# Softmax groups computed from PSUM with row sums on ScalarE, in a cross-attention kernel with a hand-written order

## The chip, the cores and the metric

The kernel runs on one core of a Trainium2 chip. The metric is device time in microseconds (us), the median over several executions. A core has five engines with a queue each: TensorE (PE in the profile; its weight loads are PEld), VectorE (DVE), ScalarE (ACT), GpSimd (POOL) and SyncE (SP), which here issues nearly all DMAs. Each queue runs in order; between engines semaphores wait for data and for buffers to come free. PE writes its results to PSUM, which has 8 banks of 128 x 512 floats; everything else lives in SBUF.

## The reference

Cross-attention with two key sets (77 text keys and 77 image keys, each with a softmax of its own), 20 heads of 32, for 2 x 2048 tokens of width 640, all in fp32:

```python
q = _split_heads(hidden_states @ Wq.T, H)
k = _split_heads(text @ Wk.T, H);     v = _split_heads(text @ Wv.T, H)
k_ip = _split_heads(ip @ Wk_ip.T, H); v_ip = _split_heads(ip @ Wv_ip.T, H)
out = _merge_heads(_attend(q, k, v, sm_scale)) + _merge_heads(_attend(q, k_ip, v_ip, sm_scale))
out = out @ Wo.T + bo
return out + residual
```

`_attend` is softmax(q k^T * sm_scale) v.

## The kernel before

The work is cut into 20 units u: 2 batches x 5 chunks of 128 channels (4 heads) x 2 halves of 1024 tokens. Two units with the same batch and chunk make a pair, numbered 0 to 9. A unit's 8 token tiles fall into three softmax groups s: groups 0 and 1 of three tiles (3 tiles x 4 heads x 2 key sets = 24 softmax rows of 77 for each token), group 2 of two tiles (16 rows). The text writes (u, s) for a group.

For each unit and 512 tokens PE projects the queries (`queries`, L197, into one bank) and ACT takes them out (L207). For each group PE computes the scores (`scores`, L229) into one half of PSUM: four banks, one for each head. Then follow, word for word of the order below:

- K: ACT copies the four banks to `pb` in SBUF (`take`, L241), after which the half is free.
- M: DVE takes the row maxima (`maxima`, L268 from SBUF, L271 from PSUM).
- S: POOL subtracts them from the rows (`subtract`, L282); E: ACT takes the exponential of the whole group in one instruction (`exponential`, L288).
- Groups in `BIASED` leave S out: the maxima are negated, and ACT takes each row by itself with its maximum as the bias (`exponential_of`, L257), 24 or 16 instructions. Groups in `DIRECT` (one before) leave K out too: maxima and exponentials read PSUM.
- D: DVE sums the rows (L295) and takes reciprocals (L297); N: POOL multiplies (`normalise`, L302); T: DVE transposes in blocks of 32 (L309).

Then PE attends for the pair (A, `attend`, L318, into one half), and ACT takes the result to `aT` (L341, L345). Keys and values of each chunk are projected (k and v, `project_kv`, L138), the values transposed by DVE (SQ, L148) and spread over `v4` by 2 x 8 small DMAs (VS, L154). The output projection of batch 0 runs under the attention of batch 1: seven block products for each 512 tokens (m1 to m7, `product`, L476 and L486, added by DVE into `acc`, L501 and L507, words cm) and a last chunk of 128 channels (o, L457, added into `res`, L467). `acc` and `res` are loaded with the residual (SF), filled and stored (SS), once for each 512 tokens. Batch 1 has a scheme of 33 products at the very end (F, L830), with weights and token sums made by DVE and POOL (V and X, L810 and L816) and results added by DVE (Y, L774 and L776).

Nothing schedules this at build time. `SCHEDULE` is one long string of words; `emit` issues each word's instructions in turn, so the words of one engine stand in its queue in that order. In `R1.13@0` the part before the dot is the word and group, then comes the unit, then the PSUM half; for q, k, v, o, p, m and F the number after @ is a bank. LX loads a block of x (1,280 KB) into one of three buffers and waits for the queries that read it, LQ and LK load weights, LO the output weights `wo_ct`. All of these are in SP's queue. The DMAs use eight semaphores in turn, so a DMA can also wait for the one issued eight before it.

Of the kernel before, what the change touches and what calls it, by code (L numbers as in the profile page):

```python
# [9 lines left out]
F32 = mybir.dt.float32  # L10
# [10 lines left out]
def kernel(  # L21
# [43 lines left out]
        (1, 2),  # L65
    }
    BIASED = {
        (1, 0), (2, 2), (3, 2), (5, 2), (6, 2), (8, 2), (9, 2), (10, 2), (11, 2), (12, 0), (12, 2), (13, 2),
        (14, 2), (15, 1), (15, 2), (16, 2), (17, 2), (18, 2), (19, 2),
# [149 lines left out]
    def rows_of(u, s):  # L219
        return keys_of(u, s).rearrange("p n g (t l) -> p (n g) t l", l=L)  # L220
# [29 lines left out]
    def exponential_of(u, s, ps=None):  # L250

        n = GROUPS[s][1]
        for g in range(G):
            for t in range(n):
                for x in range(2):
                    row = rows_of(u, s)[:, t * G + g, x]
                    nc.scalar.activation(  # L257
                        row,
                        row if ps is None else rows_in(ps[g], n)[:, t, x],
                        AF.Exp,  # L260
                        bias=maxs[(u, s)][:, t * G + g, x : x + 1],
                    )
# [29 lines left out]
    def sums(u, s):  # L292
        n = GROUPS[s][1] * G
        den = small.tile([P, n, 2], F32, tag=f"den{n}", name=f"den_{u}_{s}")
        nc.vector.tensor_reduce(den, rows_of(u, s), AX.X, ALU.add)  # L295
        rden = small.tile([P, n, 2], F32, tag=f"rden{n}", name=f"rden_{u}_{s}")
        nc.vector.reciprocal(rden, den)  # L297
        rdens[(u, s)] = rden
# [241 lines left out]
    for t in range(2):  # L540
# [75 lines left out]
    def emit(word):  # L616
# [24 lines left out]
        elif k == "SF":  # L641
            fetch(x, PARTS[y])
        elif k == "SS":
            store(x, PARTS[y])
        elif k[0] in "KMSEDNT":
            ps = at[f"R{i}.{x}"]
            if k[0] == "K":
                take(x, i, ps)
# [224 lines left out]
```

## Time and profile before

| what | us |
|---|---|
| median of 3 runs | 503.95 (503.49 to 506.41) |
| the profiled execution | 506.55 |
| its span, first to last instruction | 504.8 |

The profile is that of one execution. Each engine's busy time is given with its share of the span; a group of instructions is named by its line in the kernel, with the tile written and the tile read, the number of instructions, their busy time together, the mean time of one, and the idle time before them with what ended it. On PE an fp32 matmul shows as two instructions. The mean time of one instruction is from its start to its end; where neighbours overlap, busy time divided by the count is less, and that is what a queue of them takes. The chain of waits goes back from the last instruction to whatever released each step.

DVE's other large items, beside those that the prediction quotes, are the transposes (115.7 us in all), POOL's the normalisation (176.1) and the subtraction (128.3).

### The profile page before, as it was taken

The page shows a single profiled execution, that of the slowest core. Times are in us where ns is not written, and L with a number is a line of the kernel's source. Part 1 is how long each engine was busy: PE and PEld are TensorE (multiplying, and loading weights), DVE is VectorE, ACT ScalarE, POOL GpSimd, SP SyncE. Part 2 cuts the span into 40 slices and gives each one's busy share as a digit, 9 for nine tenths or more (in the row PEclk, how much of TensorE's full clock was granted, in tenths as well). Part 3 has the DMA queues.
Part 4 walks back from the last instruction along what each step waited for, and adds up shares of the span by engine and source line. Part 5 has one row for each costly group of instructions (what it writes and reads, how often), then busy time and mean ns, then how long its engine had stood idle before and what let it go on. Part 6 is the DMA issues. An engine that isn't in the chain of part 4 may idle for free.

```text
span 504.8 us, 10180 instructions
## 1 busy us (share of the span) xinstructions
PE 494.1 (98%) x4114; PEld 290.5 (58%) x4114; DVE 431.5 (85%) x397; ACT 299.0 (59%) x743; POOL 379.8 (75%) x163
## 2 busy tenths in 40 slices
PE   8999999999999999999999999999999999999996
PEld 4657567648557556456566556555665675443442
DVE  0069999989998999869999899788899989898985
ACT  1169788768787589658786947586786354100000
POOL 0069588998898887789886888459789979797530
PEclk9999999999999999999999999999999999999999
DMA  8981351230491471885423773454545104310125
GB/s 268 354 223 43 93 138 39 70 84 12 133 259 38 126 254 31 283 297 187 133 62 93 228 255 99 149 178 147 181 133 174 43 2 147 126 62 22 42 93 199
DMA packets 67471, 69.37 MB, mean 137 GB/s; under 512 B 5472, under 2 KB 47200, under 8 KB 67424
## 3 DMA queue, kind: packets, MB, share of 16 engines
q1 hardware_dynamic: 66704, 68.00, 43.2%
q8 instruction: 32, 0.52, 0.4%
q10 hardware_dynamic: 720, 0.72, 0.4%
q14 instruction: 15, 0.12, 0.1%
HBM read 54.94 MB, written 10.49 MB: 130 GB/s over the span
## 4 chain that ended last, share of the span: by engine, by line
PE 82%; DMA 10%; DVE 3%; SPq 3%; issue 1%; ACT 1%; DVEq 0%
PE bank L197 29%; PE bank L318 10%; PE bank L476 9%; PE bank L830 9%; PE bank L229 9%; PE bank L138 8%; PE bank L457 6%; DMA wo_ct<-in_L_xattn_Wo_dram 3%; PE bank L486 3%; DMA out_dram<-res 2%; DMA aT<-in_L_xattn_Wk_ip_dram 2%; DMA wq<-in_L_xattn_Wq_dram 1%; DMA x<-in_x_dram 1%; DVE x L776 1%; SPq L154 1%
## 5 line engine op out<-in xcount | busy, mean ns | idle before, releaser
L302 POOL TENSOR_TENSOR pb<-pb,rden 128x1848 f32<-128x1848 f32 (+1 forms) x60 | 176.1, 2942 | 36.8 <-DVE rden L297 34.9
L197 PE MATMUL bank<-x,wq 128*128 128x512 f32 x400 | 180.8, 601 | 1.3 <-DMA x<-in_x_dram 1.1
L282 POOL TENSOR_TENSOR pb<-pb,mx 128x1848 f32<-128x1848 f32 (+1 forms) x40 | 128.3, 3210 | 52.0 <-DVE mx L268 51.8
L268 DVE TENSOR_REDUCE mx<-pb 128x24 f32<-128x1848 f32 (+1 forms) x59 | 108.2, 1845 | 33.3 <-ACT pb L241 33.1
L197 PEld LDWEIGHTS bank<-x,wq 128*128 128x128 f32 x400 | 74.0, 191 | 88.0 <-issue 81.4
L295 DVE TENSOR_REDUCE den<-pb 128x24 f32<-128x1848 f32 (+1 forms) x60 | 110.4, 1840 | 14.9 <-ACT pb L288 13.8
L309 DVE STREAM_TRANSPOSE pb<-pb 128x1920 f32<-128x1920 f32 (+1 forms) x60 | 115.7, 1931 | 5.2 <-POOL pb L302 4.7
L241 ACT COPY pb<-bank 128x462 f32<-128x462 f32 (+1 forms) x236 | 100.2, 533 | 32.9 <-PE bank L229 32.3
L288 ACT ACTIVATE pb<-pb 128x1848 f32<-128x1848 f32 (+1 forms) x40 | 68.4, 1714 | 34.0 <-POOL pb L282 33.8
L257 ACT ACTIVATE pb<-pb,mx 128x77 f32<-128x77 f32 x328 | 84.0, 356 | 6.8 <-DVE mx L268 6.7
L229 PEld LDWEIGHTS bank<-kT,qT 32*128 32x128 f32 x1280 | 46.2, 184 | 24.9 <-issue 16.0
L229 PE MATMUL bank<-kT,qT 32*128 32x154 f32 x1280 | 57.6, 306 | 0.5 <-ACT kT L545 0.3
L318 PE MATMUL bank<-pb,v 32*32 32x512 f32 x1600 | 56.7, 597 | 0.9 <-issue 0.7
L138 PEld LDWEIGHTS bank<-wo_ct,aT 128*128 128x128 f32 x320 | 43.4, 188 | 5.5 <-issue 4.6
L138 PE MATMUL bank<-wo_ct,aT 128*128 128x154 f32 x320 | 45.9, 296 | 0.1
L318 PEld LDWEIGHTS bank<-pb,v 32*32 32x32 f32 x1600 | 31.5, 103 | 22.4 <-issue 10.3
L207 ACT ACTIVATE qT<-bank 128x512 f32<-128x512 f32 x40 | 23.7, 600 | 32.9 <-PE bank L197 32.9
L457 PE MATMUL bank<-aT,wo_ct 128*128 128x512 f32 x80 | 36.4, 597 | 0.1
L476 PE MATMUL bank<-aT,wo_ct 128*128 128x256 f32 x128 | 32.6, 387 | 1.2 <-DVE acc L507 1.2
L476 PEld LDWEIGHTS bank<-aT,wo_ct 128*128 128x128 f32 x128 | 23.5, 190 | 10.3 <-issue 5.0
L776 DVE TENSOR_TENSOR x<-x,bank 128x512 f32<-128x512 f32 x36 | 23.7, 681 | 4.9 <-PE bank L830 4.5
L457 PEld LDWEIGHTS bank<-aT,wo_ct 128*128 128x128 f32 x80 | 14.9, 190 | 17.0 <-issue 16.5
(74 smaller groups left out, 370.3 us busy)
## 6 DMA issues: line engine op xcount, KB each, us to landing
x<-in_x_dram SPq DMA_DIRECT2D x20, 1280.0 KB, 7.7
out_dram<-acc SPq DMA_DIRECT2D x20, 256.0 KB, 2.8
x<-in_x_dram SPq DMA_DIRECT2D x18, 256.0 KB, 5.9
acc<-in_x_dram SPq DMA_DIRECT2D x16, 256.0 KB, 3.8
out_dram<-x SPq DMA_DIRECT2D x15, 256.0 KB, 2.1
v<-vS SPq DMA_DIRECT2D x160, 20.0 KB, 2.4
wq<-in_L_xattn_Wq_dram SPq DMA_DIRECT2D x9, 320.0 KB, 6.8
aT<-in_L_xattn_Wk_dram SPq DMA_DIRECT2D x5, 512.0 KB, 5.4
```

The source lines that it names most:

```text
L138: nc.tensor.matmul(keys_in(out), loaded[n][:, k, :], cT[:, k, :, t, :], start=(k == 0), stop=(k == NCC - 1))
L197: nc.tensor.matmul(pq, wqs[q % 3][:, k, :], xs[place_of(u, h)][:, k, :], start=(k == 0), stop=(k == NC - 1),)
L229: nc.tensor.matmul(ps[g][:, ts(t, 2 * L)], qTs[(u, h)][g * D : (g + 1) * D, ts(st, P)], kT[g * D : (g + 1) * D, c, b].rearrange("p t l -> ...
L241: nc.scalar.copy(keys_of(u, s)[:, :, g], ps[g][:, : n * 2 * L].rearrange("p (n l) -> p n l", n=n))
L257: nc.scalar.activation(row, row if ps is None else rows_in(ps[g], n)[:, t, x], AF.Exp, bias=maxs[(u, s)][:, t * G + g, x : x + 1],)
L268: nc.vector.tensor_reduce(mx, rows_of(u, s), AX.X, ALU.max, negate=negate)
L282: nc.gpsimd.tensor_tensor(rows_of(u, s), rows_of(u, s), maxs[(u, s)].unsqueeze(3).to_broadcast([P, n, 2, L]), ALU.subtract)
L295: nc.vector.tensor_reduce(den, rows_of(u, s), AX.X, ALU.add)
L302: nc.gpsimd.tensor_tensor(rows_of(u, s), rows_of(u, s), rdens[(u, s)].unsqueeze(3).to_broadcast([P, n, 2, L]), ALU.mult)
L309: nc.vector.transpose(p, p)
L318: nc.tensor.matmul(pa[r][g * D : (g + 1) * D, :], v4s[q % 2][rows, g, k, :], zones[rows, :, g, k, :], start=(k == 0), stop=(k == NK - 1),)
L476: nc.tensor.matmul(part, w_of[m][:, kp, op], t_of(m, b, i)[:, kp], start=(op == kp == 0 and m in (1, 2, 5)), stop=(op == 1 and kp == 1 and ...
```

## The change

`DIRECT` grows from one group to ten, all in units 11 to 18; `BIASED` shrinks from 19 groups to 11; and a new set, `SUMMED`, names 11 of these 21 groups whose row sums come out of the exponentials themselves: each L267 instruction gets `accum_out`, which writes the sum of its 77 results. These groups have no D. The reciprocal becomes a word of its own, I (`invert`), for all 60 groups. Line numbers shift by 2 to 16.

```diff
     DIRECT = {
-        (1, 2),
+        (11, 0), (12, 0), (13, 0), (13, 2), (14, 0), (14, 2), (15, 1), (15, 2), (16, 2), (18, 1),
     }
     BIASED = {
-        (1, 0), (2, 2), (3, 2), (5, 2), (6, 2), (8, 2), (9, 2), (10, 2), (11, 2), (12, 0), (12, 2), (13, 2),
-        (14, 2), (15, 1), (15, 2), (16, 2), (17, 2), (18, 2), (19, 2),
+        (3, 2), (4, 0), (5, 2), (6, 2), (8, 2), (9, 2), (10, 2), (11, 2), (12, 2), (18, 2), (19, 2),
+    }
+    SUMMED = {
+        (10, 2), (12, 0), (12, 2), (13, 0), (13, 2), (14, 0), (15, 1), (16, 2), (18, 1), (18, 2), (19, 2),
     }
...
-    def exponential_of(u, s, ps=None):
+    def exponential_of(u, s, ps=None, den=None):
...
                     nc.scalar.activation(
                         row,
                         row if ps is None else rows_in(ps[g], n)[:, t, x],
                         AF.Exp,
-                        bias=maxs[(u, s)][:, t * G + g, x : x + 1],
+                        bias=maxs[(u, s)][:, *one],
+                        accum_out=None if den is None else den[:, *one],
                     )
...
     def sums(u, s):
+        nc.vector.tensor_reduce(den_of(u, s), rows_of(u, s), AX.X, ALU.add)
+
+    def invert(u, s):
         n = GROUPS[s][1] * G
-        den = small.tile([P, n, 2], F32, tag=f"den{n}", name=f"den_{u}_{s}")
-        nc.vector.tensor_reduce(den, rows_of(u, s), AX.X, ALU.add)
         rden = small.tile([P, n, 2], F32, tag=f"rden{n}", name=f"rden_{u}_{s}")
-        nc.vector.reciprocal(rden, den)
+        nc.vector.reciprocal(rden, dens[(u, s)])
...
     SCHEDULE = (
-        "R0.0@1 K0.0 M0.0 LK.4 LK.5 S0.0 R1.0@0 K1.0 M1.0 S1.0 R2.0@1 K2.0 M2.0 S2.0 q.1.1@1 q.1.0@6 v.0.1@0 E0.0 "
...
+        "R0.0@1 R1.0@0 K0.0 q.1.0@4 K1.0 M0.0 M1.0 S0.0 R2.0@0 v.0.0@7 K2.0 cq.1.0 S1.0 M2.0 E0.0 v.0.1@3 LK.6 "
...
     ).split()
```

All of `SCHEDULE` is new. PE's words are the same 231 in both, in another order and partly in other banks; so are the loads and stores, and the words V and X of the last stage are partly moved between DVE and POOL. The three places at which the prediction needs the new order are shown there: PE at the start, SP around A.4 (`VS.4.1 VS.5.1 LO` now follow `LX.12.0 LX.12.1`; before, the order was `LX.12.0 LO VS.4.0 LX.12.1`), and ACT around the group (13, 0).

Between the scores of a direct group and the next use of the banks that they fill, PE's words are now:

```text
R0.11@1  m2.0 o.0                      R1.11@1
R0.12@0  q.13.1 m6.0 q.14.0            A.5@0
R0.13@0  m7.0 q.14.1 m4.0              R1.13@0
R2.13@1  o.1                           m1.1@5 (one bank)
R2.14@0  q.16.0                        R1.14@0
R0.14@0  q.15.1 q.15.0                 A.6@0
R2.15@0  m6.1 q.16.1                   R1.15@0
R1.15@0  m7.1 q.17.0 m4.1 m2.2 R1.16   R0.16@0
R2.16@0  m1.2 q.18.0                   A.7@0
R1.18@0  o.3 q.19.1 m4.2               A.8@0
```

More of the change, by code (lines that the diff above doesn't have):

```diff
@@ L248, in rows_in, with den_of @@
         return ps[:, : n * 2 * L].rearrange("p (n t l) -> p n t l", n=n, t=2)
-    def exponential_of(u, s, ps=None):
+    dens = {}
+    def den_of(u, s):
+        n = GROUPS[s][1] * G
+        dens[(u, s)] = small.tile([P, n, 2], F32, tag=f"den{n}", name=f"den_{u}_{s}")
+        return dens[(u, s)]
+    def exponential_of(u, s, ps=None, den=None):
         n = GROUPS[s][1]
@@ L256, in exponential_of @@
                     row = rows_of(u, s)[:, t * G + g, x]
+                    one = t * G + g, slice(x, x + 1)
                     nc.scalar.activation(
@@ L644, in emit @@
             store(x, PARTS[y])
-        elif k[0] in "KMSEDNT":
+        elif k[0] in "KMSEDINT":
             ps = at[f"R{i}.{x}"]
@@ L653, in emit @@
                 elif direct or biased:
-                    exponential_of(x, i, ps if direct else None)
+                    exponential_of(
+                        x, i, ps if direct else None, den_of(x, i) if (x, i) in SUMMED else None
+                    )
                 else:
@@ L657, in emit @@
             else:
-                dict(S=subtract, D=sums, N=normalise, T=transpose)[k[0]](x, i)
+                dict(S=subtract, D=sums, I=invert, N=normalise, T=transpose)[k[0]](x, i)
         elif k == "q":
```

122 rows, old and new, of the table SCHEDULE are left out of this document.

## The prediction

> **What bounds the kernel now.** I read the page first, for the engines' shares; then the chain of waits, for the price of each kind of work on TensorE; then the waits of PE, and the timeline where they fall.
>
> ```profile
> PE 494.1 (98%) x4114; PEld 290.5 (58%) x4114; DVE 431.5 (85%) x397; ACT 299.0 (59%) x743; POOL 379.8 (75%) x163
> x<-in_x_dram SPq DMA_DIRECT2D x20, 1280.0 KB, 7.7
> ```
>
> PE is busy nearly throughout, so the end moves only by the PE work or by the gaps in it. The chain of waits (start, length, what) prices the work:
>
> ```profile
> 25.59 2.77 ACT pb L241 x6
> 28.40 8.85 PE bank L197 x20
> ...
> 43.65 4.29 PE bank L197 x10
> 47.94 2.11 PE bank L138 x16
> 50.05 0.74 PE bank L229 x16
> 50.78 4.49 PE bank L197 x10
> ...
> 63.39 1.00 PE bank L229 x24
> ...
> 70.98 5.45 PE bank L318 x154
> ...
> 190.29 2.63 DMA v<-vS
> ...
> 201.62 13.02 DMA wo_ct<-in_L_xattn_Wo_dram
> ...
> 214.66 0.51 SPq L154
> ...
> 215.26 6.36 DMA x<-in_x_dram
> ...
> 232.64 0.43 PE bank L486 x2
> 233.07 0.86 PE bank L476 x4
> ...
> 310.88 8.10 DMA out_dram<-res
> 319.04 3.01 DMA res<-in_x_dram
> 322.15 0.75 DVE res L467
> ...
> 414.84 3.43 PE bank L457 x8
> ...
> 446.26 14.61 PE bank L830 x34
> ...
> 500.82 0.69 DVE x L776
> ```
>
> One query projection (q) costs 4.29, one key or value projection 2.11, a group's scores (R) 1.00 or 0.74, an attend (A) 5.45, an output chunk 4.29 (ten instructions like a q) or 3.43, L476, L486 and L830 0.215, 0.215 and 0.43 an instruction. A full-array piece straight behind scores or an attend takes 0.2 more (4.49 against 4.29). From the first scores on the schedule holds 37 q (158.7), 18 projections (38.0), 60 R (54.8), 10 A (54.5), 4 o and 4 p (30.9), 4 z (3.4), 288 instructions of L476 and L486 (61.9) and 132 of L830 (56.8): 459, and 50 changes from scores or attend to full array, 10: 469. Before and after hold the same pieces and, counted in their PE order, the same 50 changes. The timeline has the first scores at 24.5, the chain the last addition at 500.8: 476.3, so 7.4 us are gaps. PE's waits (total, times, longest), and then the timeline (start, length, what, the wait before it), say where:
>
> ```profile
> PE bank L476 <- DVE acc L507: 1.2, 1, 1.2
> PE bank L830 <- DVE pb L810: 1.2, 1, 1.2
> ...
> PE bank L318 <- issue: 0.7, 1, 0.7
> ...
> PE bank L830 <- DVE x L776: 0.3, 1, 0.3
> ```
>
> ```profile
> 24.48 3.81 PE L229 MATMUL bank<-kT,qT 32*128 32x154 f32 x64 [0.31 <-ACT kT L545]
> ...
> 182.89 5.50 PE L318 MATMUL bank<-pb,v 32*32 32x512 f32 x159
> ...
> 209.24 4.56 PE L197 MATMUL bank<-x,wq 128*128 128x512 f32 x10
> 213.73 1.07 PE L229 MATMUL bank<-kT,qT 32*128 32x154 f32 x24
> 214.95 6.40 PE L318 MATMUL bank<-pb,v 32*32 32x512 f32 x160 [0.15 <-DMA v<-vS]
> 221.76 4.53 PE L197 MATMUL bank<-x,wq 128*128 128x512 f32 x10 [0.42 <-DMA x<-in_x_dram]
> ```
>
> The first three score groups take 3.9 (24.48 to 28.40) for 2.74 of work: 1.15 of gap, in which the chain runs through ACT's copies (25.59). A.4 loses 0.15 and 0.9 (6.40 against 5.50), the q behind it 0.42; a product waits 1.2 at 323; the last stage 1.5. That names 6.1 of the 7.4.
>
> **The change part by part.** On PE at the start, of before, from the middle of the third score group (banks 71 to 74):
>
> ```order
> L229 MATMUL bank_71<-kT,qT_1_153 128x154
> L229 MATMUL bank_72<-kT,qT_1_153 128x154
> L229 MATMUL bank_73<-kT,qT_1_153 128x154
> L229 MATMUL bank_74<-kT,qT_1_153 128x154
> L197 MATMUL bank_68<-x_85,wq_75 128x512 x5
> L197 MATMUL bank_73<-x_84,wq_75 128x512 x5
> L138 MATMUL bank_67<-wo_ct,aT 128x154 x8
> ```
>
> And of after, from the last score of the second group (bank 70):
>
> ```order
> L231 MATMUL bank_70<-kT,qT_1_153 128x154
> L199 MATMUL bank_71<-x_84,wq_75 128x512 x5
> L231 MATMUL bank_67<-kT,qT_1_153 128x154
> L231 MATMUL bank_68<-kT,qT_1_153 128x154
> L231 MATMUL bank_69<-kT,qT_1_153 128x154
> ```
>
> A q now stands ahead of the third group: 4.29 us against the 4 copies that must empty its banks. The q itself needs one copied bank, 0.5 us after the first group, while the second group's 1.0 runs. So -1.15.
>
> On SyncE around A.4 (x_83 and x_84 are blocks for the q behind it, v the values for A.4, wo_ct the output weights), of before:
>
> ```order
> L445 DMA res<-in_x_dram 128x512
> L182 DMA x_83<-in_x_dram 128x5x512
> L160 DMA wo_ct<-in_L_xattn_Wo_dram 128x5x640
> L154 DMA v_0_80<-vS_0_93 32x160 x8
> L182 DMA x_84<-in_x_dram 128x5x512
> L182 DMA x_82<-in_x_dram 128x5x512
> ```
>
> and of after:
>
> ```order
> L190 DMA wq_75<-in_L_xattn_Wq_dram 128x5x128
> L184 DMA x_83<-in_x_dram 128x5x512
> L184 DMA x_84<-in_x_dram 128x5x512
> L156 DMA v_0_80<-vS_0_93 32x160 x8
> L156 DMA v_1_81<-vS_95 32x160 x8
> L162 DMA wo_ct<-in_L_xattn_Wo_dram 128x5x640
> ```
>
> In before the last copy of v issues at 214.66, when wo_ct has landed, and x_84 behind it at 215.26; that is the gap of 1.47. Both now stand ahead of wo_ct. The price: x_84 issues once q.11.0, which reads its buffer, ends, 11.7 us of PE work before A.4 (two q 8.58, scores 2.74, changes 0.4). If the last v copy again waits for the big load ahead of it, it goes out at 7.7 (the page's landing time), takes 0.5 to issue and 2.6 to land: 0.9 to spare. wo_ct issues behind 8 more copies of 0.6, 13 us after q.11.0, and is first read 22.9 after it. Its 1.6 MB took 13.0 with 1.3 MB of x just ahead of it, so about 7 alone: 2 to 3 to spare. So -1.5; if the cover is gone, the same 1.5 comes back here.
>
> The product's wait at 323 hangs on res (stored, 8.10, then reloaded, 3.01) behind x blocks. SyncE now stores and reloads it further ahead of its use, so -1.2. The last stage keeps its 1.5: same products, other sequence, no better reason.
>
> The groups need their prices per engine (busy, mean):
>
> ```profile
> L257 ACT ACTIVATE pb<-pb,mx 128x77 f32<-128x77 f32 x328 | 84.0, 356 | 6.8 <-DVE mx L268 6.7
> L257 ACT ACTIVATE pb<-bank,mx 128x77 f32<-128x77 f32 x16 | 3.6, 382 | 0.0
> L271 DVE TENSOR_REDUCE mx<-bank 128x4 f32<-128x308 f32 x4 | 1.6, 455 | 0.0
> L295 DVE TENSOR_REDUCE den<-pb 128x24 f32<-128x1848 f32 x40 | 82.2, 2056 | 11.3 <-ACT pb L288 11.3
> L295 DVE TENSOR_REDUCE den<-pb 128x16 f32<-128x1232 f32 x20 | 28.2, 1409 | 3.6 <-ACT pb L288 2.6 <-ACT pb L257 1.0
> ```
>
> ACT around (13, 0) in before: qT is a query tile, L241 the copies that empty banks, L288 the exponential of a group at once:
>
> ```order
> L207 ACTIVATE qT_1_2437<-bank_72 128x512
> L241 COPY pb<-bank_67 128x3x154
> L241 COPY pb<-bank_68 128x3x154
> L241 COPY pb<-bank_69 128x3x154
> L241 COPY pb<-bank_70 128x3x154
> L241 COPY pb<-bank_71 128x2x154
> L241 COPY pb<-bank_72 128x2x154
> L241 COPY pb<-bank_73 128x2x154
> L241 COPY pb<-bank_74 128x2x154
> L288 ACTIVATE pb<-pb 128x12x154
> ```
>
> and in after:
>
> ```order
> L267 ACTIVATE pb,den_0_2401<-bank_67,mx_0_2396 128x77 x6
> L267 ACTIVATE pb,den_0_2401<-bank_68,mx_0_2396 128x77 x6
> L267 ACTIVATE pb,den_0_2401<-bank_69,mx_0_2396 128x77 x6
> L267 ACTIVATE pb,den_0_2401<-bank_70,mx_0_2396 128x77 x6
> L209 ACTIVATE qT_1_2455<-bank_73 128x512
> L209 ACTIVATE qT_0_2462<-bank_74 128x512
> ```
>
> The group's copies are gone; its banks stay full until the maxima (DVE) and 24 exponentials are through. Maxima from PSUM: 4 x 0.4 for 16 rows, times 2056/1409 (the same reduction's two sizes) for 24: 1.6 and 2.3. A row from PSUM 3.6/16 = 0.225, from SBUF 84.0/328 = 0.256. With 0.2 for two hand-overs a direct group holds its half 5.4 (16) or 7.9 us (24), plus its rows times **a**, the unknown price of a row sum. PE's cover until the half is needed (0.25 more until its last bank): (11,0) m2.0, o.0 7.3; (12,0) 10.8; (13,0) 9.0; (14,2) one q 4.7; (14,0) two q 9.0; (15,2) 6.5; (16,2) 6.5; (18,1) 11.6; (15,1) 12.6. For (13,2) the product behind o.1 needs its second bank alone, and that fits. Without a, (11,0) overruns by 0.6 and (14,2) by 0.7: +1.3.
>
> For a the trace of before shows nothing. From 0 (the sum rides along) to 0.256 (a second instruction like the row); below 0 is excluded, the same row runs. A row takes 356 ns by itself and 256 in the run, so losing the overlap costs 0.10. I take half of that, 0.05: (13,0) and (14,0) then overrun by 0.1 each, +0.2. At 0.10 it is +3.1, at 0.256 +21.
>
> The Trainium skill, ScalarE: Activation LUTs, section Rules for kernel authors, budgets about 0.3 us for an ACTIVATE with a pointer bias plus 0.83 ns an element, which speaks against row by row. By it, an estimate, a row would be 0.36, the overruns would sum to 14 and the kernel would take about 514. The trace disagrees (0.256 and 0.225 in the run), since neighbours overlap, so this gets no chance of its own.
>
> Off the path: DVE loses 11 sums (5 x 2.06 + 6 x 1.41 = 18.7) and gains 2.4 for maxima from PSUM; ACT loses the copies of ten groups. Neither is what PE waits for, so they count nothing. The reciprocals stay 60; one of a summed group now waits for ACT's last row, and behind that of (13, 0), for one, stand a product's addition, a transpose and the maxima of (13, 2) in DVE's queue, for which ACT's next rows and PE's q.16.0 wait. A late row passes its delay to them (rival 2).
>
> Sum on the profiled execution's 506.55 (span 504.8): -1.15 - 1.5 - 1.2 + 1.3 + 0.2 = 504.2. The median of the runs (503.95) lies 2.6 under that execution: 501.6.
>
> **The rivals.** 1. *Row sums are dear* (slower): the read-out is an instruction of its own on ACT, PSUM halves stay full, PE waits at (13,0), (14,0), (16,2), (12,0), (18,1). At a = 0.256: 501.4 + 21 = 522; slower by 1% from a = 0.16 on. For: five covers are within 1 to 4 us of the hold. Against: only five places. The Trainium skill, VectorE: DVE Perf Modes, section Two Vector instructions with no wait between them, says that an op that writes its accumulator is two instructions, of VectorE; no run here shows it yet.
>
> 2. *DVE comes late.* Until A.4 no sum leaves DVE, which is as full as before:
>
> ```profile
> 40.00:60.00 20.00, 20.00 (x163) 13.76 (x156) 19.47 (x21) 18.65 (x62) 13.70 (x5) 1.00 0.25 69
> ```
>
> With 0.5 of 20 free, one transpose or maximum in the wrong place delays an attend or a copy-out; about 1 us at five attends: 506.5, slower than 509 only at 1.5 each. For: every queue is reordered. Against: the same load ran with gaps of 0.7 before.
>
> 3. *Nearly all gaps close* (faster): 506.55 - 7.4 - 2.6 = 496.5 at best, 498.5 with 2 us of gaps left. For: the named gaps are order, not work. Against: the last stage's waits have the same cause as before.
>
> **How the numbers follow.** Forecast 0.42 (own range 499 to 504), rival 1 0.18, rival 2 0.17, rival 3 0.23. About 1% is what a measurement of this kernel tells from no change: 498.9 and 509. Faster: rival 3 and the forecast's edge, 0.25. Slower: most of rival 1, a fourth of rival 2, 0.19. The rest 0.56. The range 496.5 to 510 holds rival 3 and the forecast; it leaves out rival 1 beyond a = 0.17 and the worst of rival 2, 0.16 together.
>
> **What would show it.** Right: PE's first three score groups end without a wait on L241; A.4 takes 5.5; L267 rows with sums run at 0.28 to 0.30; waits of PE's scores on L267 sum to 1 to 2. Wrong: rows with sums at 0.4 or more (rival 1), attends waiting for L309's transposes (rival 2), a v copy or wo_ct landing late at A.4 or m2.0.

## The result, and the profile after

The changed kernel takes 500.36 us (median of 15 runs, 498.81 to 503.98), the kernel before on the same chip 504.54 (15 runs, 503.44 to 506.48): 0.9917 of it, 95% interval 0.9897 to 0.9937. The profiled execution took 503.08 with a span of 501.3. The page's busy times, of the changed kernel:

```profile
PE 492.2 (98%) x4114; PEld 290.7 (58%) x4114; DVE 410.7 (82%) x409; ACT 306.8 (61%) x970; POOL 376.5 (75%) x166
```

VectorE has 21 us less to do than before, ScalarE 8 more. The timeline of PE (start, length, what, and in brackets the wait before it), at the places of which the prediction spoke:

```profile
23.55 1.96 PE L231 MATMUL bank<-kT,qT 32*128 32x154 f32 x48 [0.31 <-ACT kT L557]
25.43 4.56 PE L199 MATMUL bank<-x,wq 128*128 128x512 f32 x10
29.92 0.81 PE L231 MATMUL bank<-kT,qT 32*128 32x154 f32 x16
...
187.03 0.58 PE L231 MATMUL bank<-kT,qT 32*128 32x154 f32 x7 [2.38 <-issue]
187.54 6.06 PE L140 MATMUL bank<-wo_ct,aT 128*128 128x154 f32 x32
...
215.30 5.52 PE L330 MATMUL bank<-pb,v 32*32 32x512 f32 x160
220.75 4.56 PE L199 MATMUL bank<-x,wq 128*128 128x512 f32 x10
...
226.95 1.13 PE L488 MATMUL bank<-aT,wo_ct 128*128 128x256 f32 x4 [0.65 <-DMA wo_ct<-in_L_xattn_Wo_dram]
...
327.97 1.99 PE L488 MATMUL bank<-aT,wo_ct 128*128 128x256 f32 x8
```

The third score group at the start goes straight through behind a q. The attend A.4 (215.30) takes 5.52 and the q behind it has no wait. The product that waited 1.2 for `acc` has none (327.97). What is left is a stop of 2.38 in the middle of a score group, for which the records name no cause, slow projections behind it (6.06 for 32 instructions, 4.48 in an undisturbed execution, below), 0.65 for `wo_ct`, and, not shown here, 0.38 for kT at 57. The view of PE's waits has none for a row of a direct group (L267). The chain of waits, of the changed kernel, ends so:

```profile
203.94 9.47 DMA x<-in_x_dram
...
219.77 7.14 DMA wo_ct<-in_L_xattn_Wo_dram
...
448.55 48.99 PE bank L846 x114
497.56 0.69 DVE acc L792
```

In the last 49 us the chain is PE's own work. From the first scores to the last addition there are 497.56 - 23.55 = 474.0 us, 5.0 over the 469 of work by the prediction's count (7.4 before); 2.38 + 1.58 + 0.65 + 0.38 are those 5.0. The stop is no fixed part of the kernel: two more executions with a profile (below) had 1.00 and 0.63 there, and the projections at full speed.

### The profile page after: what moved, and what is told of

Same layout as the page of the kernel before. It is cut to its first block, busy times and chain, and to the rows that moved or that the text cites. A ratio compares the mean times of both kernels' runs of the same rounds, so it can differ in the third digit from the quotient of the medians.

```text
span 501.3 us, 10439 instructions
## 1 busy us (share of the span) xinstructions
PE 492.2 (98%) x4114; PEld 290.7 (58%) x4114; DVE 410.7 (82%) x409; ACT 306.8 (61%) x970; POOL 376.5 (75%) x166
## 4 chain that ended last, share of the span: by engine, by line
PE 90%; DMA 6%; SPq 2%; issue 1%; DVE 0%; ACT 0%
PE bank L199 30%; PE bank L846 11%; PE bank L488 10%; PE bank L231 10%; PE bank L330 10%; PE bank L140 9%; PE bank L469 7%; PE bank L498 3%; DMA x<-in_x_dram 2%; DMA aT<-in_L_xattn_Wk_ip_dram 2%; DMA wq<-in_L_xattn_Wq_dram 1%; DMA wo_ct<-in_L_xattn_Wo_dram 1%; SPq L156 1%; SPq L532 1%; SPq L130 0%
## 5 line engine op out<-in xcount | busy, mean ns | idle before, releaser
L293 POOL TENSOR_TENSOR pb<-pb,mx 128x1848 f32<-128x1848 f32 (+1 forms) x39 | 121.7, 3129 | 60.4 <-DVE mx L279 55.3
L279 DVE TENSOR_REDUCE mx<-pb 128x24 f32<-128x1848 f32 (+1 forms) x50 | 91.4, 1843 | 31.6 <-ACT pb L243 31.5
L243 ACT COPY pb<-bank 128x462 f32<-128x462 f32 (+1 forms) x200 | 85.3, 540 | 42.2 <-PE bank L231 41.8
L304 DVE TENSOR_REDUCE den<-pb 128x24 f32<-128x1848 f32 (+1 forms) x49 | 91.5, 1878 | 15.6 <-ACT pb L299 11.9
L299 ACT ACTIVATE pb<-pb 128x1848 f32<-128x1848 f32 (+1 forms) x39 | 65.4, 1680 | 17.2 <-POOL pb L293 17.0
L267 ACT ACTIVATE pb<-bank,mx 128x77 f32<-128x77 f32 x208 | 59.1, 390 | 12.3 <-DVE mx L282 12.2
L330 PE MATMUL bank<-pb,v 32*32 32x512 f32 x1600 | 55.2, 597 | 0.0
L267 ACT ACTIVATE pb<-pb,mx 128x77 f32<-128x77 f32 x184 | 52.7, 357 | 1.1 <-DVE mx L279 0.8
L267 ACT ACTIVATION_READ_ACCUMULATOR pb<-bank,mx 128x1 f32 x152 | 40.2, 273 | 0.0
L488 PEld LDWEIGHTS bank<-aT,wo_ct 128*128 128x128 f32 x128 | 23.6, 190 | 8.3 <-issue 4.0
```

What stands on the lines that cost most here:

```text
L243: nc.scalar.copy(keys_of(u, s)[:, :, g], ps[g][:, : n * 2 * L].rearrange("p (n l) -> p n l", n=n))
L267: nc.scalar.activation(row, row if ps is None else rows_in(ps[g], n)[:, t, x], AF.Exp, bias=maxs[(u, s)][:, *one], accum_out=None if den i ...
L279: nc.vector.tensor_reduce(mx, rows_of(u, s), AX.X, ALU.max, negate=negate)
L293: nc.gpsimd.tensor_tensor(rows_of(u, s), rows_of(u, s), maxs[(u, s)].unsqueeze(3).to_broadcast([P, n, 2, L]), ALU.subtract)
L304: nc.vector.tensor_reduce(den_of(u, s), rows_of(u, s), AX.X, ALU.add)
L330: nc.tensor.matmul(pa[r][g * D : (g + 1) * D, :], v4s[q % 2][rows, g, k, :], zones[rows, :, g, k, :], start=(k == 0), stop=(k == NK - 1),)
```

## The experiments

Times are medians; ratios are to the kernel before on the same chip, with their 95% intervals. The changed kernel itself was run twice more among them.

| kernel | us | ratio |
|---|---|---|
| 1: before, three moves of the change | 511.64 | 1.0141 (1.0113 to 1.0169) |
| 2: changed, without the row sums | 505.32 | 1.0015 (0.9996 to 1.0034) |
| 3: changed, direct rows in reverse | 511.88 | 1.0141 (1.0114 to 1.0169) |
| 4: changed, again | 498.90 | 0.9884 (0.9858 to 0.9910) |
| 5: changed, without direct groups | 527.33 | 1.0439 (1.0403 to 1.0475) |
| 6: changed, one load of x later | 498.63 | 0.9888 (0.9870 to 0.9906) |
| 7: as 1, and W0 later | 505.93 | 1.0027 (1.0006 to 1.0048) |
| 8: changed, another load of x later | 505.28 | 1.0023 (1.0003 to 1.0043) |
| 9: before, with 11 row sums | 508.96 | 1.0094 (1.0073 to 1.0115) |
| 10: as 7, with 11 row sums | 512.44 | 1.0145 (1.0123 to 1.0168) |
| 11: changed, a third time | 499.50 | 0.9895 (0.9879 to 0.9911) |
| 12: as 6, and a projection later | 498.91 | 0.9890 (0.9872 to 0.9907) |

### 1 and 7. The order alone

The prediction took three waits away by order alone, so the three moves were made in the kernel before.

```diff
-R2.0@1 K2.0 M2.0 S2.0 q.1.1@1 q.1.0@6
+q.1.0@4 R2.0@0 K2.0 M2.0 S2.0 q.1.1@1
-LX.12.0 LO VS.4.0 LX.12.1
+LX.12.0 VS.4.0 LX.12.1 LO
 SS.1.4 and SF.2.4 moved behind VS.6.1 and VS.7.0
```

> The kernel before with three moves alone: the query projection q.1.0 ahead of the third score group, VS.4.0 and LX.12.1 ahead of the output weights on SyncE, and the store and reload of res for the third 512 tokens further ahead. Theory (the gain is the order at a few places): the first three score groups lose their 1.15 us, A.4 and the q behind it 1.5, the product at 323 its 1.2: 3 to 4 us under before, ratio 0.992 to 0.994, and PE's waits on DMA and on DVE acc L507 are gone from the profile. Rival (the gain is the row sums and the direct groups, which take work off DVE): under 1 us, ratio above 0.998, and other waits come up at the same places.

It became 7 us slower. The first of the two views is PE's timeline in this kernel, the second POOL's:

```profile
229.31 3.36 PE L229 MATMUL bank<-kT,qT 32*128 32x154 f32 x24 [4.75 <-ACT aT L341]
```

```profile
219.94 1.26 POOL L387 TENSOR_TENSOR x<-wo_ct 128x512 f32<-128x512 f32 x1 [7.91 <-issue]
...
223.72 6.52 POOL L282 TENSOR_TENSOR pb<-pb,mx 128x1848 f32<-128x1848 f32 x2
```

POOL stands 7.9 us ahead of the word W0 (L387, sums of two blocks of `wo_ct`) and only then subtracts for the tenth unit (L282). The POOL line names no cause; the load of `wo_ct` was issued at 210.15 and landed 9.7 later, at 219.85, just ahead of W0. ACT's exponential waits for that, and behind it in ACT's queue stands the copy of A.4's result (L341), for whose bank PE waits 4.75. The change has W0 behind these subtractions. Run 7 moves that one word (its third move is again the store and reload of `res`, not additions of the last stage as its text has it):

```diff
-W0 S0.10 E0.10 ... S1.10 E1.10
+S0.10 E0.10 ... S1.10 W0 E1.10
```

> The kernel before with the three moves that made it slower (a query group ahead of the third score group, wo_ct's load behind two more loads and eight copies of v, the last stage's two additions later), and one more: GpSimd's sum of two blocks of wo_ct (W0) stands behind the two subtractions of its tenth block rather than ahead of them, as the change has it. A: the 4.75 us wait at 229 came from GpSimd standing at that sum until wo_ct landed: the wait goes, and with it the low clock behind it; the time is 3 to 4.5 us below the kernel before, ratio 0.991 to 0.994. B: the lateness comes from elsewhere (ScalarE's own order): a wait of 3 us or more stays at score group R0.11 and the kernel is slower than before.

The wait at 229 went, so that cause is shown. But nothing was gained: 1.0027. PE's timeline, of run 7:

```profile
31.43 4.56 PE L197 MATMUL bank<-x,wq 128*128 128x512 f32 x10 [0.81 <-ACT pb L241]
...
234.87 0.81 PE L229 MATMUL bank<-kT,qT 32*128 32x154 f32 x16 [2.18 <-DVE acc L501]
```

A.4 (5.52), the q behind it and the product at 323 now run without a wait, but part of what was taken out is back in another place: 0.81 at the start, where the next q needs a bank that ACT's copies have not emptied, and 2.18 for VectorE, whose addition of a product (L501) is late and holds the banks of a score group. The last stage's waits of 1.2 (L829 for L809) and 0.3 are where they were.

### 2. Without the row sums

```diff
-    SUMMED = {(10, 2), (12, 0), ..., (19, 2)}
+    SUMMED = set()                                (and D ahead of I for these 11 groups)
```

> The changed kernel with SUMMED empty: DVE sums the rows of the 11 groups again, right ahead of their reciprocals, 18.7 us more on DVE in units 10 to 19, and ACT loses 216 read-outs (about 18 us). Theory (PE is the bound and DVE has 1 to 6 us free in each 20 there): within 1 us of the changed kernel, ratio to before 0.990 to 0.994. Rival (the sums on ACT are what the change gains): 4 us or more above the changed kernel, ratio 0.999 or more, with attends waiting for L321's transposes.

5 to 6 us slower than the changed kernel (500.36, and 498.90 in the same set of runs), and level with before. Of run 2, a stretch of DVE's timeline and then of PE's (line numbers are 2 lower than in the changed kernel):

```profile
276.10 2.07 DVE L302 TENSOR_REDUCE den<-pb 128x24 f32<-128x1848 f32 x1
...
278.43 0.78 DVE L511 SCALAR_TENSOR_TENSOR acc<-bank,bo_sb,acc 128x256 f32<-128x256 f32 x2
```

```profile
279.26 0.80 PE L229 MATMUL bank<-kT,qT 32*128 32x154 f32 x14 [0.70 <-DVE acc L511]
```

VectorE is 429.2 busy instead of 410.7. A sum that is back in its queue (L302) stands ahead of the additions into `acc` (L511) that free banks for PE's scores, and PE waits 0.70. The new waits are mostly of this kind: 1.9 us for `acc`, 0.73 for a copy of queries by ACT, 0.3 for a transpose, so the attends were not what suffered. They sum to 2.9 of the 5.1 us by which this span is longer than that of run 4; PE's busy time has grown by another 2.9, and the wait for `wo_ct` is 1.1 shorter. That VectorE is off the path in the new order is refuted. The order was written for groups without a sum; other words were not moved to make room for the 11 sums.

### 3. The direct rows in reverse

ACT takes the banks of a direct group last first, so that its first row needs the last of VectorE's four maxima.

```diff
-        for g in range(G):
+        for g in range(G) if ps is None else reversed(range(G)):
```

> The changed kernel, but in a direct group ACT takes the heads in reversed order, so its first row needs the last of DVE's four maxima, and the bank that PE wants first is emptied last. Theory (ACT's rows start behind the first maximum, so three of four maxima hide under the rows; that is why the overruns forecast at (11,0) and (14,2) did not come): a hold of 24 rows grows by 1.9 us, of 16 rows by 1.4; PE then waits about 1 us each at (11,0), (13,0), (14,0), (13,2), (14,2), (16,2): 5 to 7 us above the changed kernel, with PE waits on ACT L267. Rival (PE's cover there is longer than thought, or other waits lie behind it): under 1.5 us more.

It cost 13 us against the changed kernel in the same set (run 4), twice what was expected. PE's waits of run 3:

```profile
PE bank L488 <- ACT pb L267: 3.2, 2, 2.1
PE bank L231 <- ACT pb L267: 2.6, 3, 1.1
```

With a third of 1.1 the waits for L267 sum to 6.9. Waits for qT and without a named cause add 3.7, of which 1.3 is a stop at 185 that the changed kernel has too. The edit does two things at once: ACT starts later (it waits 24.9 us in all for the maxima of direct groups, 12.2 in the changed kernel), and the banks come free in reverse, the one that PE wants first as the last. So the 13 us are the price of both together. The views of the changed kernel show how the hand-over runs there: PE's, DVE's and ACT's timelines around the group (13, 0).

```profile
269.05 0.92 PE L231 MATMUL bank<-kT,qT 32*128 32x154 f32 x17
270.16 0.54 PE L231 MATMUL bank<-kT,qT 32*128 32x154 f32 x7 [0.20 <-issue]
...
279.44 1.84 PE L231 MATMUL bank<-kT,qT 32*128 32x154 f32 x40
```

```profile
270.66 2.27 DVE L282 TENSOR_REDUCE mx<-bank 128x6 f32<-128x462 f32 x4 [3.61 <-PE bank L231]
```

```profile
271.33 0.33 ACT L267 ACTIVATE pb<-bank,mx 128x77 f32<-128x77 f32 x1 [0.87 <-DVE mx L282]
271.56 0.19 ACT L267 ACTIVATION_READ_ACCUMULATOR pb<-bank,mx 128x1 f32 x1
...
278.25 0.45 ACT L267 ACTIVATE pb<-bank,mx 128x77 f32<-128x77 f32 x1
...
278.55 1.21 ACT L209 ACTIVATE qT<-bank 128x512 f32<-128x512 f32 x2
```

And ACT's timeline at a direct group without sums, (11, 0):

```profile
227.07 5.27 ACT L267 ACTIVATE pb<-bank,mx 128x77 f32<-128x77 f32 x24
```

The four maxima take 2.27, but the first row starts 0.67 after the first of them, and the other three lie under the rows. The 24 rows with sums take 278.55 - 271.33 = 7.22, 0.301 a row; without sums 5.27, 0.22. The banks are held from 270.7 to 278.7, 8 us, and the next scores in them start at 279.44.

### 4 and 11. The changed kernel again

> The changed kernel once more, as a control beside the others. Ratio 0.990 to 0.994. Its profiled execution had a PE stop of 2.4 us in a score group at 184.7, without a releaser, and a granted clock of 0.91 in 180 to 200. Theory (that stop is an accident of one execution, which took 503.1 against a median of 500.4): the stop is gone or much shorter here, the granted clock in 180 to 200 is 1.00 and the execution takes 499 to 501. Rival (it comes from this order, as when instructions are fetched while the DMA engines are full): the stop comes back at the same place, 1.5 us or more.

> The changed kernel once more, as the measure for the next run on the same chip: 0.988 to 0.992 of before; a stop of TensorE at about 185 of 1 us or more, a wait for wo_ct at m2.0 of 0.6 to 1.5.

498.90 and 499.50, the same as the first measurement within the intervals. PE's timeline of run 4 shows how much the two remaining gaps change from one execution to the next:

```profile
185.05 0.54 PE L231 MATMUL bank<-kT,qT 32*128 32x154 f32 x7 [1.00 <-issue]
185.52 4.48 PE L140 MATMUL bank<-wo_ct,aT 128*128 128x154 f32 x32
...
224.18 1.13 PE L488 MATMUL bank<-aT,wo_ct 128*128 128x256 f32 x4 [1.48 <-DMA wo_ct<-in_L_xattn_Wo_dram]
```

In run 11 they are 0.63 and 0.41.

### 5. Without the direct groups

```diff
-    DIRECT = {(11, 0), (12, 0), ..., (18, 1)}
+    DIRECT = set()               (the ten groups in BIASED instead, K ahead of M for each)
```

> The changed kernel, but its ten groups whose exponentials read PSUM are copied to SBUF by ScalarE first, as the other 40 are, and their rows read SBUF; the 11 groups' row sums and the order stay. A: reading PSUM buys ScalarE time (ten groups' four copies, 40 x 0.54 = 21.6 us, and 208 rows at 0.256 in place of 0.22, 7.5 us), and ScalarE's lateness shows on TensorE, as the 11 row sums did: slower than the changed kernel by 1 to 4 us, with new waits of score groups or products on ScalarE or VectorE. B: ScalarE has the room (307 of 501 us busy), and the direct groups only hold their banks longer: within 0.7 us of the changed kernel, or faster.

27 us slower than the changed kernel, seven times what was expected. Of this kernel, PE's waits, then PE's and ACT's timelines at the same group (13, 0):

```profile
PE bank L230 <- ACT qT L208: 3.9, 2, 3.0
PE bank L487 <- DVE acc L518: 3.3, 2, 1.7
PE bank L230 <- DVE acc L512: 2.4, 1, 2.4
```

```profile
269.70 2.54 PE L230 MATMUL bank<-kT,qT 32*128 32x154 f32 x24
```

```profile
273.14 1.87 ACT L242 COPY pb<-bank 128x462 f32<-128x462 f32 x4
277.15 0.36 ACT L266 ACTIVATE pb<-pb,mx 128x77 f32<-128x77 f32 x1 [2.14 <-DVE mx L278]
...
285.03 0.34 ACT L266 ACTIVATE pb<-pb,mx 128x77 f32<-128x77 f32 x1
```

The reciprocals, from the groups by line, of this kernel and then of the changed one:

```profile
L308 DVE RECIPROCAL rden<-den 128x24 f32<-128x24 f32 (+1 forms) x60 | 16.0, 273 | 16.8 <-ACT pb L266 15.9
```

```profile
L309 DVE RECIPROCAL rden<-den 128x24 f32<-128x24 f32 (+1 forms) x60 | 15.9, 272 | 4.9 <-ACT pb L267 4.0
```

And of this kernel DVE's timeline behind the last row of (13, 0), then PE's:

```profile
285.50 0.30 DVE L308 RECIPROCAL rden<-den 128x24 f32<-128x24 f32 x1 [3.34 <-ACT pb L266]
285.72 0.78 DVE L512 SCALAR_TENSOR_TENSOR acc<-bank,bo_sb,acc 128x256 f32<-128x256 f32 x2
```

```profile
286.55 0.88 PE L230 MATMUL bank<-kT,qT 32*128 32x154 f32 x14 [2.35 <-DVE acc L512]
```

ACT is 329.1 busy, 22 more than in the changed kernel, and over the whole span still idle for a third of it. But between 240 and 320 it is busy for 17.0 to 18.4 of each 20 us, and from 268 to 300 the chain of waits runs through its rows (49%) and copies (19%). What counts is the way of one group: the copies are followed by one maximum over all 24 rows, and only then by rows at 0.343 each. From the end of the scores to the last exponential this takes 13.1 us, in the changed kernel 8.0. VectorE's queue stands at the reciprocal of a summed group until the last row is done: 15.9 us in all, in the changed kernel 4.0. Behind it stand additions that free PE's banks: the lines above show one such chain, from the row to the reciprocal (3.34), the addition and PE's scores (2.35). The run holds for this order, which was written for direct groups: other words were not moved to suit the copies.

### 6, 8 and 12. Loads of x later

Run 6 moves a load of 1,280 KB (LX.10.1) behind eight copies of v, run 8 another one (LX.12.1) behind `wo_ct`. Run 12 is run 6 with v.1.0 and its copy behind k.1.0.

```diff
 run 6:   -LX.10.1 D2.8 ... VS.5.0          +D2.8 ... VS.5.0 LX.10.1
 run 8:   -LX.12.1 VS.4.1 ... VS.5.1 ... LO +VS.4.1 ... VS.5.1 ... LO LX.12.1
 run 12:  -v.1.0@3 ... k.1.1@6 ... k.1.0@7  +k.1.1@6 ... k.1.0@7 v.1.0@5
```

> The changed kernel, with one load of 1280 KB of x (LX.10.1) issued behind eight copies of v, so that fewer large transfers fall on 176 to 187 us, where TensorE stopped for 2.4 and 1.0 us in two executions of the changed kernel with nothing to wait for in the records. A: the stop is TensorE's instruction blocks arriving late behind 99% busy DMA engines: the stop goes to under 0.3 us or moves to where the DMA engines are then full, and the time is 0.7 to 1.5 us shorter. B: the stop belongs to that place in the program: it stays at 1 us or more, time within 0.5 us. Both: if the load is needed sooner than it lands, a wait on DMA x appears at the query group of the twelfth block pair, and the time is longer.

> The changed kernel with one load of x (LX.12.1) issued behind wo_ct's load rather than ahead of the 16 copies of v, which stood 3 us at the landing of that load and passed it on to wo_ct (the chain of waits: 9.5 us DMA x, eight or nine copies at 0.59, wo_ct 7.1, product). A: wo_ct lands 2 to 3 us sooner, the product's wait of 0.65 to 1.5 us goes: 0.6 to 1.5 us below the changed kernel. B: that block of x then lands too late for its query group at 221 us, and the wait only changes its place: within 0.5 us, or slower.

> The changed kernel with the load of x behind eight copies of v, which took the stop at 185 and the wait for wo_ct down to 0.65 and 0, and with the projection v.1.0 behind k.1.0, so that kT's copy runs under it rather than ahead of the score group R2.2 (wait 0.38). A: both gaps are free to go: 0.986 to 0.989 of before, 0.5 to 2 us below the changed kernel on this chip; span 496 with no gap but the first 1.1 and a stop under 0.7. B: what was won at 185 and 227 in the one profile was the execution's luck: within 0.5 us of the changed kernel.

In run 6 the stop is 0.65 and the wait for `wo_ct` is gone; in run 12 they are 0.34 and 0.24, the wait for kT is gone, and a wait of 0.76 for an addition (L519) is new. The spans of these two executions are the shortest, 496.3 and 496.7. But the medians, 498.63 and 498.91, are not told apart from 498.90 and 499.50 of the changed kernel: run 12 lies 0.6 under run 11 on the same chip, well inside both intervals. Both beat the kernel before by 1.1%; that they beat the changed kernel is not shown. Run 8 is clear. PE's timeline:

```profile
219.97 6.23 PE L199 MATMUL bank<-x,wq 128*128 128x512 f32 x10 [3.40 <-DMA x<-in_x_dram]
```

The load lands too late for its q, and 3.4 us of wait for x replace 0.4 to 1.5 for `wo_ct`; the q itself then takes 6.23 instead of 4.56.

### 9 and 10. Row sums in the order of before

Run 9 is the kernel before with 11 of its own row-by-row groups summed by ScalarE, run 10 the same with the moves of run 7. They are not the 11 groups of the change: ten have 16 rows and all read SBUF, 184 rows against 216.

```diff
+    SUMMED = {(10, 2), (11, 2), (12, 0), (12, 2), (13, 2), (14, 2), (15, 2), (16, 2), (17, 2), (18, 2), (19, 2)}
 D becomes I for these groups, D I for all others   (DIRECT and BIASED as before)
```

> The kernel before, its order and its groups, but 11 of its row-by-row groups in units 10 to 19 take their row sums from the exponentials (no D for them; the reciprocals stay where they stood). A: the gain needs both, VectorE's relief and the new places of a few words; the waits of before at the start, at A.4 and at the product stand in the order and stay: 0.997 to 1.001 of before. B: VectorE's relief alone is what the change gains: 0.990 to 0.994.

> The kernel before with the 11 row sums of the run above and the four moves of the run in which the sum over wo_ct stood later (which by themselves moved the gaps to VectorE: 2.2 at 235 and 1.7 in the last stage, and gained nothing). A: with VectorE relieved these gaps go: 0.990 to 0.994 of before, as the whole change, and the ten groups read from PSUM are then no condition of the gain in this order. B: ScalarE, which now carries sums and copies, comes late as it did in the changed kernel without its direct groups: over 1.003, waits on ScalarE's qT or pb of 3 us or more.

Both are slower than before, run 9 by 4.3 us and run 10 by 7.8, so neither theory of run 9 held; of run 10's, B had the time, but not its sign of 3 us or more in waits for ScalarE (qT and pb have 1.0 in the view). VectorE is relieved to 416.6, ACT loaded to 315.4. The waits listed for PE hardly grew in run 9; they are inside the busy time. PE's score groups, by line, first of run 9, then of run 6:

```profile
L232 PE MATMUL bank<-kT,qT 32*128 32x154 f32 x1280 | 61.1, 306 | 0.6 <-ACT kT L558 0.3 <-ACT aT L358 0.2
```

```profile
L231 PE MATMUL bank<-kT,qT 32*128 32x154 f32 x1280 | 56.6, 306 | 1.3 <-issue 0.6 <-ACT kT L684 0.4 <-ACT kT L557 0.3
```

The mean of one is the same 306, the time together is 4.5 longer (in the kernel before it is 57.6): the instructions of a group no longer follow each other closely, because bank after bank is late. PE's and ACT's timelines at the longest of them, of run 9:

```profile
269.11 2.65 PE L232 MATMUL bank<-kT,qT 32*128 32x154 f32 x24 [0.19 <-ACT aT L358]
```

```profile
262.45 0.38 ACT L268 ACTIVATE pb<-pb,mx 128x77 f32<-128x77 f32 x1
...
267.94 0.60 ACT L210 ACTIVATE qT<-bank 128x512 f32<-128x512 f32 x1
268.42 2.24 ACT L358 COPY aT<-bank 128x256 f32<-128x256 f32 x8
```

16 rows with sums take 267.94 - 262.45 = 5.49, 0.343 a row, against 0.256 before, and the copies of an attend's result (L358) stand 1.4 us longer behind them. PE's 24 scores need the banks one by one as the copies empty them: 2.65 instead of 1.07. Here the sums make ACT late at the copies; in run 10 the wait of 2.2 for the addition at 235 stayed besides.

## Why the prediction held, step by step

The forecast was 501.6, the result 500.36, inside the forecast's own range. The size was less right than that looks: the sum was -2.35 and 501.6 is 0.9953 of the 503.95 it started from; measured were -4.2 and 0.9917, in the repeats 0.9884 and 0.9895, and 0.9953 lies outside all three intervals. The loss of 1.5 that the sum forecast did not come and the last stage gave 1.5 more; a stop and a wait for `wo_ct` that it did not have took part of that back. That the time still fell within the range is in part luck. The steps one by one:

- **Three score groups at the start, -1.15: right.** 23.55 to 30.73 without a wait on the copies.
- **A.4 and the q behind it, -1.5: right, but barely; the spare of `wo_ct` was wrong.** The last copy of v for A.4 went out at 213.43 and landed in 1.7, 0.2 ahead of A.4, where 0.9 was forecast: the x block ahead of it took longer (9.47, not 7.7), and the copy's shorter way (1.7 from its issue, where 0.5 and 2.6 were put) made up for most of that. `wo_ct` got 2 to 3 us of spare; it lacks 0.65, 1.48 and 0.41 in three executions. The load itself took 7.14, as estimated ("about 7"). The issue was put 13 us behind q.11.0, and came 15.8 behind (203.94 to 219.77): the x block took 9.47, where the 7.7 was the profile page's median, and the copies of v behind it with their gaps took 6.4.
- **The product's wait at 323, -1.2: right.** It is gone.
- **"The last stage keeps its 1.5": wrong.** It went. In runs 7, 9 and 10, with before's order of the last stage, 1.2 and 0.3 are still there; in the changed order no run shows them. That points to the sequence of the last stage, which I had not costed for want of a reason. It is not shown: run 1, in before's sequence and late by then, does not have these waits either.
- **Direct groups, +1.3: wrong, the hold was mis-sized.** I added the four maxima in full, two hand-overs and the rows: 7.9 for 24 rows without sums, 9.1 with the a that I took. Measured are 8.0 with sums. Three of the four maxima run under the rows, and the hold is nearer to 0.7 plus the rows. Run 3, which puts the maxima back in front and also frees the banks in reverse, costs 13 us; how much of that is the overlap alone was not separated.
- **Row sums, a = 0.05: mis-sized.** 0.301 against 0.22 from PSUM: a = 0.08. From SBUF 0.343 against 0.256: 0.087. That is nearly the 0.10 of "losing the overlap", which by my sum would have cost 3; with the true hold it costs PE nothing. Rival 1's mechanism, a second instruction for each row, is what the trace shows, at a third of its price. The sentence of the Trainium skill cited with it (VectorE: DVE Perf Modes, section Two Vector instructions with no wait between them), which speaks of VectorE, fits ScalarE here too.
- **"Neither is what PE waits for, so they count nothing": wrong.** This is the step that failed most, although it did not show in the sum. Taking VectorE's relief back costs 5 to 6 us (run 2), taking ScalarE's relief back 27 (run 5, in which the way of each group is longer as well). The mechanism is that of rival 2, a late row passed on through the reciprocal to additions and banks, and run 5 shows it at work.
- **The signs.** The first two came. Rows with sums ran at 0.301 from PSUM, at the upper end. Waits on L267 of 1 to 2 did not come, and one sign of being wrong did: `wo_ct` landing late at m2.0.
- **The gaps of before.** The ones that the prediction lists add up to 5.3; its 6.1 has to count the 0.7 of the line L318 <- issue too.

The gaps closed by order did not come free, then. Run 7 has the moves without the relief: nothing gained. Runs 9 and 10 have the sums without the direct groups: ScalarE late, 4 and 8 us lost. The changed order without sums: nothing gained; without direct groups: 23 us lost. Of the combinations tried, only all of it together gives 4 us or more; the order of before with the ten direct groups, and the new order with neither, were not run. The row sums take 18.5 us from VectorE and load ScalarE with them; the direct groups take the copies from ScalarE and shorten the group's way by 5 us; and the order uses that room. I had costed the first two as loads off the path, where they are the condition of the third. Which single words of the new order are needed beside those tried was not tested.

## What to carry to other kernels

Where one engine is busy nearly throughout, the others have no value by their busy share but by when each of their results is due: price a relief by undoing it within the new order, not in the old one. If a consumer starts behind the first of several partial results, count only the first; and look for waits in the busy time too, by the busy time of a group of instructions against another run with the same count and mean. A load moved later moves every instruction that waits for it, on each engine that has other work queued behind: the place of the word W0 was worth 6 us (runs 1 and 7) that PE's own order did not show.

## What was not expected of the hardware

**The sum of a row** on ScalarE is a second instruction, ACTIVATION_READ_ACCUMULATOR, of 198 ns from SBUF and 273 from PSUM (means of the changed kernel). It overlaps with its neighbours so far that a row costs 80 to 90 ns more.

**The clock behind a wait.** The granted clock over 20 us, from the windows view (us, busy times, then clock, DMA share, GB/s), first of the changed kernel, then of run 3 and run 1:

```profile
180.00:200.00 20.00, 17.62 (x233) 12.76 (x204) 14.21 (x14) 11.99 (x33) 14.22 (x6) 0.91 0.42 126
```

```profile
180.00:200.00 20.00, 18.73 (x226) 13.27 (x206) 15.28 (x13) 13.06 (x38) 15.29 (x6) 0.91 0.43 130
```

```profile
220.00:240.00 20.00, 15.25 (x54) 8.46 (x51) 9.54 (x7) 11.53 (x27) 18.50 (x9) 0.83 0.65 220
```

Behind waits of 2.38, 3.40 (run 8) and 4.75 us the clock was 0.91, 0.91 and 0.83. The length of the wait does not settle it: behind 1.26 in run 3 the clock was 0.91 too, behind 2.18 in run 7 it stayed at 1.00, and in run 10 it was 0.91 in 260 to 280, where no wait over 0.24 is listed but a group of 24 scores is drawn out to 2.65. Where the clock fell, the wait cost more than itself: the 32 projection instructions took 6.06 behind the 2.38 and 6.14 behind the 1.26, instead of 4.48. The Trainium skill, TensorE: Matmul & The Clock Gate, section What's actually happening, has windows of about 3.4 us, half the clock after an idle one and the full clock after a busy one; by it, an estimate, one such window in 20 us gives 0.915 and two 0.83, which agrees. A stop of 1.26, which was enough in run 3, is shorter than its idle window; here the measurement decides.

**The stop at 185** falls behind the 17th score of one group in every run with the changed order: 2.38, 1.00 and 0.63 in the changed kernel, 1.16, 1.26, 1.71 and 0.52 in runs 2, 3, 5 and 8, and 0.65 and 0.34 in runs 6 and 12, where fewer bytes are on the DMA engines just then. With these bytes still there, runs 8 and 11 have 0.52 and 0.63, no longer. The Trainium skill, Runtime: NRT & Kernel Launch, section Instruction fetch mechanics, says that instructions come in blocks by DMA and that the cost of a block's end is mostly hidden; the DMA view of the changed kernel has two packets in the instruction queue between 174 and 192. Two executions with the later load are too few to settle it: the cause stays open.
